# Keys with tokens on partitions: a second read from DRAM in 32-row squares and VectorE's transpose in place of TensorE's

## The chip, the cores and the metric

The kernel runs on one core of a Trainium2 chip. The metric is the device time of one execution in microseconds; lower is better.

## The reference

A layer norm feeds two branches whose outputs are added to the input: a gated delta-rule attention and a small mixture of experts. The change lies in the attention. Cut to what matters:

```python
q = silu(causal_dwconv(x @ Wq));  k = silu(causal_dwconv(x @ Wk)) * DK ** -0.5
v = silu(causal_dwconv(x @ Wv))                        # 16 heads of 128, 2 x 2048 tokens
alpha, beta = sigmoid(x @ Wa + ba), sigmoid(x @ Wb + bb)

def step(S, inps):                                     # one token
    qt, kt, vt, at, bt = inps
    err = einsum('bhvk,bhk->bhv', S, kt) - vt
    S = at[..., None, None] * S - bt[..., None, None] * (err[..., None] * kt[:, :, None, :])
    return S, einsum('bhvk,bhk->bhv', S, qt)

o = layernorm(o) * ln_w + ln_b
o = (o * sigmoid(x @ Wg)) @ Wo
out = x + o + experts(xn)                              # xn: x after the layer norm
```

All arrays are float32.

## The kernel before

The recurrence over tokens is done in chunks of 128 tokens (`C`). A unit `u` is one batch and one pair of heads (`HG` = 2), 16 units in all. A block `n` is 512 tokens of a unit, and has four chunks `c` = 0 to 3. One chunk of one unit is called a step here; there are 16 x 16 = 256 of them. Each has three parts: `before(n, c)` prepares a chunk, `after(n, c)` carries the state `S` across it in the next step, and `output(n, c)` normalises the result one step later still.

Projection and convolution give keys, queries and values with channels on partitions and tokens along the free dimension. `kt` is the key tile of a block, 128 channels x 2 heads x 512 tokens. It was computed well ahead by `key_item`, stored to DRAM in `k_d`, and is read back by `loads`. Most products take it in that layout. The state update is the exception: `after` at L707 needs `kg`, keys with tokens on partitions, scaled for each token by `gd1`. So `before` transposes keys and values for both heads on TensorE with an identity (L640 for keys, L641 for values) into one PSUM bank `pkv`; ScalarE copies the bank to SBUF as `kv` (L649); GpSimd multiplies the key half by `gd1` into `kg` (L655). The value half goes into `r` on VectorE (L691).

Around these lines `before` also builds the inverse of a triangular matrix, in stages that alternate between TensorE (L620, L636, L658, L667) and the other engines. L629 and L631 are VectorE's copies out of the first two PSUM banks, the second with a mask (`pT`). L645 is a transpose on VectorE of a 128 x 32 tile, done in squares of 32 x 32; L646 and L652 place its results.

In `after`, L687 multiplies keys by the state, L691 gives `r`, L698 applies the inverse `inv`, L702 copies the result to `w`, L707 and L714 give the new state, and L721 and L724 write the chunk's output into PSUM. That last pool, `ps_o`, has one bank. In `output`, L748 reads the bank on VectorE, with `rs` that GpSimd computed at L735; only then can the next step's L721 write it.

The steps are interleaved by hand. In `recurrence` a sequence of `step(...)` calls advances the three parts and, between them, two items (`A`, `B`) of the projections of the next block by the plan `PLAN`: q0 and the keys of a later unit at c = 0, q1 and v0 at c = 1, g0 and keys at c = 2, v1 and g1 at c = 3. The items' matmuls are at L155, their convolution sums are three instructions each on VectorE (L141), and `qg` is made on GpSimd (L388) from `gin`, which is loaded into a single buffer (L380). `inv` steps of `inverses` run on GpSimd (L264, L267) out of `Y`, loaded at L255; `ex` steps advance the experts, in the first call of `recurrence` alone. The call is made under a manual schedule:

```python
with tc.manual_schedule(engines={E.PE, E.DVE, E.Activation, E.Pool}):
```

Those four engines run in the written order. DMAs are issued by SyncE (SP) and are placed by the framework's scheduler; each waits for the release of what it overwrites, and on one of eight completion semaphores used in turn. `load_ops` issues 22 small loads for each block (L332, L342, L346), `before` two loads into `inv` (L614), which has four buffers.

`recurrence` is called twice, once for each batch. Between the calls the output projection of the first batch runs by itself; that of the second is interleaved.

Of the kernel before, what the change touches and what calls it, by code (L numbers as in the profile page):

```python
# [7 lines left out]
F32 = mybir.dt.float32  # L8
# [3 lines left out]
ALU = mybir.AluOpType  # L12
# [3 lines left out]
P = 128  # L16
NB, T, HID = 2, 2048, 512
H, D, KS = 16, 128, 4
C = 128
# [5 lines left out]
HG = 2  # L25
NP = H // HG
NHC = HG * NC
Q = 32
NQ = C // Q
# [14 lines left out]
def block_kernel(ctx, tc, x, wq, wk, wv, wg, wo, wa, wb, ba, bb, par, consts,  # L44
                 topk_idx, topk_w, ew0, ew1, ew2, ewd0, ewd1, out):
    nc = tc.nc
# [13 lines left out]
    ident = unit[:, 1:DW]  # L60
# [22 lines left out]
    for i in range(1, NQ, 2):  # L83
# [5 lines left out]
    gd1 = [cp.tile([P, NC, H], F32, tag=f"gd1{b}", name=f"gd1{b}") for b in range(NB)]  # L89
# [25 lines left out]
    k_d = [[dp.tile([HG, P, BLK], F32, name=f"k_d{u}_{k}") for k in range(NBK)]  # L115
           for u in range(NB * NP)]
# [191 lines left out]
    def loads(n):  # L308
# [11 lines left out]
        qg = bp.tile([P, HG, BLK], F32, tag="qg", name="qg")  # L320
        have[n] = (decs, kt, qt, qg, [None] * HG, [])

    def load_ops(n):

        u, blk = blocks[n]
        op = ops[n % 2]
        for h in range(HG):
            hc = slice(h * NC + blk * CB, h * NC + (blk + 1) * CB)
            cc = slice(blk * CB, (blk + 1) * CB)

            def put(k, row, a, q=Q):
                nc.sync.dma_start(out=op[k][row:row + q, :, row:row + q], in_=a)  # L332

            def block(form, g):
                return X_d[u][form, h, g, cc, :].rearrange("c (i j) -> i c j", j=Q)

            for pr in range(2):

                lo, hi, row = 2 * pr, 2 * pr + 1, 64 * h + Q * (1 - pr)
                put("a32", row, aT_d[u][lo * Q:hi * Q, hc, hi * Q:(hi + 1) * Q])  # L340
                put("ihi", row, block(1, hi))
                nc.sync.dma_start(out=op["ilo"][row:row + Q], in_=block(0, lo))  # L342
            for g in range(2):
                row = 64 * h + Q * g
                col = Q * (2 - g)
                nc.sync.dma_start(out=op["top"][row:row + Q, :, col:col + Q], in_=block(0, g))  # L346
                put("bot", 64 * h + Q * g, block(1, 2 + g))
            put("a64", 64 * h, aT_d[u][0:64, hc, 64:C], 64)
# [226 lines left out]
    def bcast(a, n):  # L575
        return bass.AP(a.tensor, a.offset, [*a.ap, (0, n)])

    def v3(t):
        return t.rearrange("p (h j) -> p h j", h=HG)
# [6 lines left out]
    HW = HG * D  # L586
# [16 lines left out]
    def before(n, c):  # L603

        u, blk = blocks[n]
        b = u // NP
        hs = slice((u % NP) * HG, (u % NP) * HG + HG)
        decs, kt, qt, _, vs, _ = have[n]
        op = ops[n % 2]
        ci, cs = blk * CB + c, slice(c * C, (c + 1) * C)  # L610

        inv = invs[(n * CB + c) % len(invs)]
        for g in range(2):
            nc.sync.dma_start(  # L614
                out=inv[g * Q:(g + 1) * Q, :, g * Q:(g + 1) * Q],
                in_=X_d[u][1, :, g, ci, :].rearrange("h (j i) -> j h i", i=Q))


        px = bank(ps_l, "l")
        nc.tensor.matmul(px[:, 0:Q], lhsT=op["a32"][:, c, :], rhs=op["ilo"][:, c, :],  # L620
                         start=True, stop=True)

        pk = bank(ps_l, "l")
        for h in range(HG):
            nc.tensor.matmul(pk[:, h * C:(h + 1) * C], lhsT=kt[:, h, cs], rhs=qt[:, h, cs],  # L625
                             start=True, stop=True)
        yield
        xs = k2.tile([P, Q], F32, tag="xs", name="xs")
        nc.vector.tensor_copy(xs, px[:, 0:Q])  # L629
        pT = k2.tile([P, HG, C], F32, tag="pT", name="pT", bufs=3)  # L630
        nc.vector.scalar_tensor_tensor(  # L631
            pT, v3(pk[:, 0:HW]), D ** -0.5, decs[:, :, c, 1:], ALU.mult, ALU.mult)
        yield

        pz = bank(ps_l, "l")
        nc.tensor.matmul(pz[:, 0:Q], lhsT=op["ihi"][:, c, :], rhs=xs, start=True, stop=True)  # L636

        pkv = bank(ps_l, "l")
        for h in range(HG):
            nc.tensor.transpose(pkv[:, h * D:(h + 1) * D], kt[:, h, cs], ident)  # L640
            nc.tensor.transpose(pkv[:, HW + h * D:HW + (h + 1) * D], vs[h][:, cs], ident)  # L641
        yield
        top, bot = op["top"][:, c, :], op["bot"][:, c, :]
        iT = k2.tile([P, Q], F32, tag="iT", name="iT")
        nc.vector.transpose(iT, pz[:, 0:Q])  # L645
        nc.vector.scalar_tensor_tensor(  # L646
            top[:, 0:Q], pz[:, 0:Q], second[:, 0:1], top[:, 2 * Q:], ALU.mult, ALU.add)
        kv = k2.tile([P, 2, HG, D], F32, tag="kv", name="kv")
        nc.scalar.copy(kv.rearrange("p s h j -> p (s h j)"), pkv)  # L649
        for h in range(HG):  # L650
            r = 64 * h
            nc.scalar.copy(bot[r:r + Q, r + Q:r + 2 * Q], iT[r:r + Q])  # L652
            nc.gpsimd.tensor_copy(inv[0:Q, h, Q:2 * Q], iT[r + Q:r + 2 * Q])  # L653
        kg = k2.tile([P, HG, D], F32, tag="kg", name="kg", bufs=3)
        nc.gpsimd.tensor_tensor(kg, kv[:, 0], bcast(gd1[b][:, ci, hs], D), ALU.mult)  # L655
        yield
        px = bank(ps_l, "l")
        nc.tensor.matmul(px[:, 0:C], lhsT=op["a64"][:, c, :], rhs=wide(top[:, 0:64]), start=True, stop=True)  # L658
        yield
        xs = k2.tile([P, C], F32, tag="xs2", name="xs2")  # L660
        nc.vector.tensor_copy(xs, px[:, 0:C])
        for h in range(HG):
            r = slice(64 * h, 64 * h + 64)
            nc.scalar.copy(inv[64:C, h, 64:C], bot[r, r])
        yield
        pz = bank(ps_l, "l")
        nc.tensor.matmul(pz[:, 0:C], lhsT=xs, rhs=bot, start=True, stop=True)  # L667
        yield
        nc.scalar.copy(inv[0:64, :, 64:C], v3(pz[0:64, 0:C]))
        found[n, c] = (pT, kv, kg, inv)  # L670

    def after(n, c):

# [1 line left out]
        b = u // NP  # L675
        h0 = (u % NP) * HG
        _, kt, _, qg, _, _ = have[n]
        pT, kv, kg, inv = found.pop((n, c))
        ci, cs = blk * CB + c, slice(c * C, (c + 1) * C)
        S = state.get(u)  # L680

        if S is None:
            r = kv[:, 1]
        else:
            pq = bank(ps_c, "c")
            for h in range(HG):
                nc.tensor.matmul(pq[:, h * D:(h + 1) * D], lhsT=kt[:, h, cs], rhs=S[:, h, :],  # L687
                                 start=True, stop=True)
            r = k2.tile([P, HG, D], F32, tag="r", name="r")
            for h in range(HG):  # L690
                nc.vector.scalar_tensor_tensor(  # L691
                    r[:, h, :], pq[:, h * D:(h + 1) * D], gd0[b][:, ci, h0 + h:h0 + h + 1],
                    kv[:, 1, h, :], ALU.mult, ALU.add)
        yield
        yield
        pw = bank(ps_c, "c")
# [66 lines left out]
    def recurrence(b, first):  # L763
# [9 lines left out]
        def step(g):  # L773
            next(g, None)

        inv = last = hold = none
        mine = {}
        with tc.manual_schedule(engines={E.PE, E.DVE, E.Activation, E.Pool}):
            for m, at in enumerate([*steps, None, None]):
                z = after(*steps[m - 1]) if 0 < m <= len(steps) else none  # L780
# [2 lines left out]
                if at:  # L783
                    n, c = at
                    u, blk = blocks[n]
                    ci = blk * CB + c
                    if c == 0:
                        if n + 1 < n0 + NP * NBK:
                            loads(n + 1)
                            load_ops(n + 1)  # L790
                        if blk == 0:
                            for _ in inv:
                                pass
                            inv = inverses(u + 1) if u + 1 < NB * NP else none
                            step(inv)
                    a = before(n, c)
                    for i, (what, h) in enumerate(PLAN[c]):
                        if what == "k":
                            if u + 2 < NB * NP:
                                key = (u + 2, blk, h)  # L800
                                pair[i] = key_item(*key, get_xT if (u + 2) // NP == b else ahead)
                        elif n + 1 < n0 + NP * NBK:
                            pair[i] = item(n + 1, what, h)
                    if u == NB * NP - 1:

                        if ci == 1:
                            wos = load_wo(b)
                        if ci >= 4:
                            if c == 0:
                                slots.append(big())  # L810
                            for _ in last:
                                pass
                            last = out_chunk(b, ci - 4, wos, slots[ci % len(slots)])
                            step(last)
# [311 lines left out]
```

## Time and profile before

| | |
|---|---|
| Time, median of 3 runs (lowest to highest) | 3907.49 us (3904.68 to 3910.80) |
| Profiled execution: its own time, its span | 3906.37 us, 3904.3 us |
| Granted TensorE clock, mean | 0.98 |
| L640, TensorE, 128x128 | 512 of 288 ns mean |
| L641, TensorE, 128x128 | 512 of 272 ns mean |
| L649, ScalarE copy, 128x512 | 256 of 585 ns mean |
| L655, GpSimd multiply, 128x256 | 256 of 616 ns mean |
| L645, VectorE transpose, 128x32 | 256 of 211 ns mean |
| DMAs issued by SyncE | 3390 |

The span runs from the first instruction to the last. [...]

### The profile page before, as it was taken

What the parts mean: (1) busy time and instruction counts of PE and PEld (TensorE: products, weight loads), DVE (VectorE), ACT (ScalarE), POOL (GpSimd) and SP (SyncE); (2) the same over time, 40 slices, a digit from 0 to 9 for tenths busy, and PEclk for the clock granted to TensorE, in tenths of its full rate; (3) what the DMA queues carried; (4) which work ended last, traced back from release to release, by engine and by line L of the source; (5) the groups of instructions that cost most, each with busy time, mean ns of one, the idle gap of its engine ahead of it and who ended that gap; (6) DMA issues with size and microseconds to landing.
All of it is one profiled execution on the core that took longest, in us unless ns stands there. A gap on an engine that the chain in (4) does not pass through costs nothing.

```text
span 3904.3 us, 59006 instructions
## 1 busy us (share of the span) xinstructions
PE 3770.2 (97%) x18046; PEld 2461.4 (63%) x18046; DVE 2343.6 (60%) x6132; ACT 1701.5 (44%) x4027; POOL 1682.4 (43%) x3046
## 2 busy tenths in 40 slices
PE   7769999999999999999999999999999999998899
PEld 6437767677677766666654466666666666664454
DVE  5536656666666667777750177777777777763231
ACT  3424444444444445555520055555555555542110
POOL 1236546465564636363630053636363545541010
PEclk7789999999999999999999999999999999999999
DMA  4634665655666553545573435353435444342322
GB/s 133 209 98 143 185 169 154 195 158 175 168 176 172 159 178 107 143 132 169 147 240 117 120 103 137 107 139 109 132 111 139 119 127 126 103 111 72 100 75 89
DMA packets 579705, 541.36 MB, mean 139 GB/s; under 512 B 354688, under 2 KB 421760, under 8 KB 574272
## 3 DMA queue, kind: packets, MB, share of 16 engines
q1 hardware_dynamic: 557280, 456.18, 40.6%
q0 software_dynamic: 22112, 81.41, 7.1%
q8 instruction: 147, 2.41, 0.3%
q14 instruction: 166, 1.36, 0.1%
HBM read 363.69 MB, written 173.67 MB: 138 GB/s over the span
## 4 chain that ended last, share of the span: by engine, by line
PE 85%; DVE 6%; DMA 4%; issue 2%; POOL 2%; SPq 1%; ACT 1%; POOLq 0%; DVEq 0%; ACTq 0%
PE p L155 39%; PE p L892 11%; PE p L1044 4%; DVE cv L141 3%; PE o L721 3%; PE l L625 3%; PE p L205 3%; PE o L724 3%; PE c L698 3%; PE c L707 3%; PE c L687 2%; PE p L1059 2%; PE l L640 1%; PE l L658 1%; PE l L667 1%
## 5 line engine op out<-in xcount | busy, mean ns | idle before, releaser
L141 DVE SCALAR_TENSOR_TENSOR cv<-raw,prm,cv 128x512 f32<-128x512 f32 x1152 | 909.5, 790 | 106.2 <-ACT cv L136 44.1
L892 PE MATMUL p<-wo,oTf 128*128 128x512 f32 x1024 | 459.7, 604 | 26.3 <-DMA oTf<-oT_d 25.1
L155 PE MATMUL p<-xT,wq 128*128 128x512 f32 x1024 | 484.6, 596 | 0.0
L653 POOL COPY inv<-iT 32x32 f32<-32x32 f32 x512 | 103.1, 201 | 884.4 <-DVE iT L645 685.1
L155 PE MATMUL p<-xT,wg 128*128 128x512 f32 x1024 | 482.0, 594 | 0.0
L155 PE MATMUL p<-xT,wv 128*128 128x512 f32 x1024 | 481.0, 593 | 0.0
L735 POOL TENSOR_TENSOR rs<-rs,mhalf 128x2 f32<-128x2 f32 x256 | 270.2, 1055 | 485.4 <-DVE rs L734 481.1
L132 ACT COPY raw<-p 128x512 f32<-128x512 f32 x384 | 223.4, 582 | 533.2 <-PE p L155 515.0
L155 PE MATMUL p<-xT,wk 128*128 128x512 f32 x896 | 433.5, 610 | 0.0
L702 ACT COPY w<-c 128x256 f32<-128x256 f32 x256 | 95.3, 372 | 635.0 <-PE c L698 635.0
L714 DVE SCALAR_TENSOR_TENSOR S<-S,gtot,c 128x128 f32<-128x128 f32 x480 | 145.2, 344 | 356.6 <-PE c L707 342.5
L892 PEld LDWEIGHTS p<-wo,oTf 128*128 128x128 f32 x1024 | 193.9, 194 | 252.2 <-issue 223.8
L267 POOL TENSOR_TENSOR Y<-Y,t 128x30 f32<-128x30 f32 (+14 forms) x480 | 308.4, 643 | 37.2
L136 ACT ACTIVATE cv<-p,prm 128x512 f32<-128x512 f32 x384 | 300.4, 782 | 1.7
L264 POOL TENSOR_TENSOR t<-Y 128x30 f32<-128x30 f32 (+14 forms) x480 | 286.2, 596 | 8.8 <-DMA Y<-aT_d 2.3
L155 PEld LDWEIGHTS p<-xT,wq 128*128 128x128 f32 x1024 | 178.0, 192 | 135.8 <-issue 135.8
L155 PEld LDWEIGHTS p<-xT,wg 128*128 128x128 f32 x1024 | 176.8, 191 | 132.3 <-issue 132.1
L155 PEld LDWEIGHTS p<-xT,wv 128*128 128x128 f32 x1024 | 176.3, 191 | 132.0 <-issue 132.0
L691 DVE SCALAR_TENSOR_TENSOR r<-c,gd,kv 128x128 f32<-128x128 f32 x480 | 145.3, 344 | 166.2 <-PE c L687 165.1
L155 PEld LDWEIGHTS p<-xT,wk 128*128 128x128 f32 x896 | 160.6, 198 | 126.3 <-issue 126.3
L388 POOL TENSOR_TENSOR qg<-q,gin 128x512 f32<-128x512 f32 x128 | 194.1, 1516 | 98.6 <-ACT q L386 98.6
L707 PEld LDWEIGHTS c<-w,kg 128*128 128x128 f32 x1024 | 154.1, 191 | 121.4 <-issue 102.1
(172 smaller groups left out, 7145.8 us busy)
## 6 DMA issues: line engine op xcount, KB each, us to landing
row<-a_d SPq DMA_DIRECT2D x128, 258.0 KB
dec_d<-decA SPq DMA_DIRECT2D x128, 258.0 KB
decB<-dec_d SPq DMA_DIRECT2D x64, 516.0 KB
k_d<-kf SPq DMA_DIRECT2D x128, 256.0 KB
k<-k_d SPq DMA_DIRECT2D x64, 512.0 KB
gin<-gin_d SPq DMA_DIRECT2D x128, 256.0 KB
aT_d<-aTf SPq DMA_DIRECT2D x128, 256.0 KB
oT_d<-oT SPq DMA_DIRECT2D x256, 128.0 KB
```

The source lines that it names most:

```text
L132: nc.scalar.copy(raw[:, KS - 1:], ps)
L136: nc.scalar.activation(cv, ps, AF.Identity, bias=cbias(p, h0 + h), scale=tap(p, h0 + h, KS - 1))
L141: nc.vector.scalar_tensor_tensor(cv, raw[:, j:j + BLK], tap(p, h, j), cv, ALU.mult, ALU.add)
L155: nc.tensor.matmul(ps, lhsT=w[:, k, h * D:(h + 1) * D], rhs=xt[k], start=(k == 0), stop=(k == NKT - 1))
L264: nc.gpsimd.tensor_tensor(t, bass.AP(col.tensor, col.offset, [col.ap[0], (Q, j), (0, n)]), bass.AP(row.tensor, row.offset, [row.ap[0], (0, ...
L267: nc.gpsimd.tensor_tensor(Y[:, 0:j, j + 1:], Y[:, 0:j, j + 1:], t, ALU.add)
L388: nc.gpsimd.tensor_tensor(qg[:, h, :], qt[:, h, :], gin, ALU.mult)
L691: nc.vector.scalar_tensor_tensor(r[:, h, :], pq[:, h * D:(h + 1) * D], gd0[b][:, ci, h0 + h:h0 + h + 1], kv[:, 1, h, :], ALU.mult, ALU.add)
L707: nc.tensor.matmul(pss[:, h * D:(h + 1) * D], lhsT=kg[:, h, :], rhs=w[:, h, :], start=True, stop=True)
L735: nc.gpsimd.tensor_tensor(rs, rs, mhalf[:, 0:HG], ALU.pow)
L892: nc.tensor.matmul(py, lhsT=oT[:, h, :], rhs=wos[h], start=(h == 0), stop=(h == H - 1))
L1044: nc.tensor.matmul(ps[:fn, s, :], lhsT=w[f][:, s, k, :], rhs=xt[:, k, :], start=(k == 0), stop=(k == NKT - 1))
```

## The change

Keys with tokens on partitions are no longer made by TensorE. The block's keys in `k_d` are read from DRAM a second time, one chunk at a time, into a tile `kb`. For each group `g` of 32 tokens one DMA brings the four 32-channel pieces of both heads, so that the 32 partitions of the group hold channels within a piece, and the free dimension holds head, piece and token. Each square of 32 x 32 is then where it belongs, but turned; one transpose of VectorE, which turns every square by itself, gives `kg`. GpSimd scales `kg` in place. TensorE transposes values alone, and ScalarE copies half as much.

`squares` issues four DMAs per step, each of 32 KB in rows of 128 bytes. It is called two steps ahead in the written order; `kb` has four buffers. The transpose is written behind `pT`, so that it stands between L631 and the next item's instruction on VectorE. The order of the other engines' instructions is the same but for the edited lines; that of SyncE's changes, since the scheduler places the new loads among the others.

```diff
+    def squares(n, c):
+        u, blk = blocks[n]
+        kbs[n, c] = kb = bp.tile([P, HG, D], F32, tag="kb", name="kb", bufs=4)
+        for g in range(NQ):
+            o = c * C + g * Q
+            nc.sync.dma_start(
+                out=kb[g * Q:(g + 1) * Q].rearrange("r h (i j) -> r (h i) j", j=Q),
+                in_=k_d[u][blk][:, :, o:o + Q].rearrange("h (i r) j -> r (h i) j", r=Q))
+
+    kbs = {}
...
         nc.vector.scalar_tensor_tensor(
             pT, v3(pk[:, 0:HW]), D ** -0.5, decs[:, :, c, 1:], ALU.mult, ALU.mult)
+        kg = k2.tile([P, HG, D], F32, tag="kg", name="kg", bufs=3)
+        nc.vector.transpose(kg.rearrange("p h j -> p (h j)"), kbs.pop((n, c)).rearrange("p h j -> p (h j)"))
         yield
...
         for h in range(HG):
-            nc.tensor.transpose(pkv[:, h * D:(h + 1) * D], kt[:, h, cs], ident)
-            nc.tensor.transpose(pkv[:, HW + h * D:HW + (h + 1) * D], vs[h][:, cs], ident)
+            nc.tensor.transpose(pkv[:, h * D:(h + 1) * D], vs[h][:, cs], ident)
...
-        kv = k2.tile([P, 2, HG, D], F32, tag="kv", name="kv")
-        nc.scalar.copy(kv.rearrange("p s h j -> p (s h j)"), pkv)
+        v = k2.tile([P, HG, D], F32, tag="vT", name="vT")
+        nc.scalar.copy(v, v3(pkv[:, 0:HW]))
...
-        kg = k2.tile([P, HG, D], F32, tag="kg", name="kg", bufs=3)
-        nc.gpsimd.tensor_tensor(kg, kv[:, 0], bcast(gd1[b][:, ci, hs], D), ALU.mult)
+        nc.gpsimd.tensor_tensor(kg, kg, bcast(gd1[b][:, ci, hs], D), ALU.mult)
...
+        squares(*steps[0]), squares(*steps[1])
         with tc.manual_schedule(engines={E.PE, E.DVE, E.Activation, E.Pool}):
...
+                    if m + 2 < len(steps):
+                        squares(*steps[m + 2])
                     a = before(n, c)
```

In `after`, `kv[:, 1]` becomes `v`.

More of the change, by code (lines that the diff above doesn't have):

```diff
@@ L669, in before @@
         nc.scalar.copy(inv[0:64, :, 64:C], v3(pz[0:64, 0:C]))
-        found[n, c] = (pT, kv, kg, inv)
+        found[n, c] = (pT, v, kg, inv)
     def after(n, c):
@@ L677, in after @@
         _, kt, _, qg, _, _ = have[n]
-        pT, kv, kg, inv = found.pop((n, c))
+        pT, v, kg, inv = found.pop((n, c))
         ci, cs = blk * CB + c, slice(c * C, (c + 1) * C)
@@ L682, in after @@
         if S is None:
-            r = kv[:, 1]
+            r = v
         else:
@@ L692, in after @@
                     r[:, h, :], pq[:, h * D:(h + 1) * D], gd0[b][:, ci, h0 + h:h0 + h + 1],
-                    kv[:, 1, h, :], ALU.mult, ALU.add)
+                    v[:, h, :], ALU.mult, ALU.add)
         yield
```

## The prediction

> **What bounds the kernel now.** I read the profile page's busy shares first, then the chain of waits, then the two stretches that hold the change (from about 250 to 2000 us and from 2250 to 3820 us, the two calls of `recurrence`), then one step of it in order of time.
>
> ```profile
> span 3904.3 us, 59006 instructions
> PE 3770.2 (97%) x18046; PEld 2461.4 (63%) x18046; DVE 2343.6 (60%) x6132; ACT 1701.5 (44%) x4027; POOL 1682.4 (43%) x3046
> PE 85%; DVE 6%; DMA 4%; issue 2%; POOL 2%; SPq 1%; ACT 1%; POOLq 0%; DVEq 0%; ACTq 0%
> DMA packets 579705, 541.36 MB, mean 139 GB/s; under 512 B 354688, under 2 KB 421760, under 8 KB 574272
> ```
>
> TensorE is busy and also 85% of the chain that ends last. The stretches show how little it pauses where the edited code runs, at a granted clock of 1.00 and 0.99, and how much room the others have:
>
> ```profile
> core 0: us, PE busy (x) PEld busy (x) DVE busy (x) ACT busy (x) POOL busy (x), PEclk, DMA share, GB/s
> 250.00:2000.00 1750.00, 1730.08 (x9144) 1190.39 (x9143) 1143.68 (x2967) 850.12 (x2045) 916.07 (x1587) 1.00 0.56 161
> 2250.00:3820.00 1570.00, 1532.71 (x7326) 989.50 (x7325) 1016.95 (x2737) 745.32 (x1780) 678.05 (x1300) 0.99 0.40 113
> ```
>
> So a TensorE instruction less is worth its issue spacing, not its duration (starts overlap). The timeline of one step (c = 1) gives the spacing; columns are start, duration, engine, line:
>
> ```profile
> 3088.98 0.31 PE L636 MATMUL l<-xs,ihi 128*128 128x32 f32 x2
> 3089.12 0.30 PE L640 MATMUL l<-unit,k 128*128 128x128 f32 x1
> 3089.26 0.27 PE L641 MATMUL l<-unit,v 128*128 128x128 f32 x1
> 3089.38 0.27 PE L640 MATMUL l<-unit,k 128*128 128x128 f32 x1
> 3089.48 0.27 PE L641 MATMUL l<-unit,v 128*128 128x128 f32 x1
> 3089.59 1.88 PE L155 MATMUL p<-xT,wq 128*128 128x512 f32 x4
> 3091.31 0.61 PE L707 MATMUL c<-w,kg 128*128 128x128 f32 x4
> 3092.23 0.49 PE L721 MATMUL o<-w,pT 128*128 128x128 f32 x2 [0.31 <-DVE o L748]
> ```
>
> The four transposes start at 3089.12, .26, .38, .48, and the next work at .59: 0.47 us together, 0.11 us each after the first. The last row is the only place where TensorE pauses in this step: L721 needs the single output bank that VectorE's L748 empties. What VectorE did before it:
>
> ```profile
> 3088.03 0.41 DVE L631 SCALAR_TENSOR_TENSOR pT<-l,decB 128x256 f32<-128x256 f32 x1
> 3088.74 2.54 DVE L141 SCALAR_TENSOR_TENSOR cv<-raw,prm,cv 128x512 f32<-128x512 f32 x3 [0.30 <-POOL raw L131]
> 3091.20 0.20 DVE L645 STREAM_TRANSPOSE iT<-l 128x32 f32<-128x32 f32 x1
> 3091.33 0.20 DVE L646 SCALAR_TENSOR_TENSOR top<-l,second,top 128x32 f32<-128x32 f32 x1
> 3091.46 0.71 DVE L748 TENSOR_SCALAR o<-o,mv,rs 128x128 f32<-128x128 f32 x2
> ```
>
> The new instruction comes right behind L631, ahead of all of these; there is 0.30 us of idle time to take some of it up.
>
> **The change part by part.**
>
> *Removed from TensorE.* 2 transposes (L640) in each of 256 steps. The pair that stays costs the first's 0.14 and one 0.11, so 0.47 falls to 0.25: 0.222 us x 256 = 56.8 us, all on the path. [...]
>
> *ScalarE.* L649 copies 128x256, not 128x512: by L702 (the same copy out of PSUM, 372 ns) against 585 ns, 0.21 us less per step. ScalarE waits for TensorE anyway; worth 0 on the path, but the copies of L652 behind it come that much sooner. *GpSimd.* L655 keeps its size (616 ns) and now waits for VectorE's earlier write rather than for ScalarE; nothing uses kg before L707 of the next step, some 10 us later. 0.
>
> *Added on VectorE.* One 128x256 f32 transpose SBUF to SBUF per step. No row has that size. From below: it could hide wholly (0), if idle time covers it. Near rows: L711, a 128x256 copy out of PSUM, 425 ns; L631, 421 ns; L645, the 128x32 transpose, 211 ns against 180 ns for the 128x32 copy L629, so a square costs about 31 ns more to fill. I take 0.45 us, of which 0.08 overlaps the next start as in neighbouring rows: 0.37 us of occupancy. From above: eight squares at 211 ns each, one after another, 1.69 us (1.6 of occupancy). [...]
>
> *What that does to L721.* For every step I took from the timeline the idle time between L631 and L748, and the slack between L748's end and L721's start (0.06 us of it is the hand-over). Median slack is 1.44 us at c = 0, 0.25 at c = 1 (a tenth have none), 1.18 at c = 2 and 3; idle time averages 0.24 at c = 1, 0.05 to 0.17 at c = 2 and 3, and all is covered at c = 0. TensorE comes 0.222 earlier, so a step gains max(-0.222, delay of L748 - slack). Summed over the steps: occupancy 0.24 us gives -48.7 us, 0.37 gives -44.1 (of it -13.6, -3.9, -13.0, -13.6 for c = 0 to 3), 0.54 about -37, 0.70 -28.5, 1.0 -1, 1.6 +75. VectorE then waits for TensorE at L714 and L661 in most steps (342.5 and 137.6 us in all), so its delay isn't carried over.
>
> *Added on SyncE.* 4 DMAs per step, 1024 more beside 3390. Mean issue is 0.434 us, so 1.7 us per step of about 12, 445 us in all; its issues now take 1473 us of the span. The other queues keep their order but for the edit; SyncE's changes, the squares standing among the loads, often eight together behind a block's 22 small loads. A square waits only for the transpose four steps earlier, which nothing holds up for long. Laying the changed order over the trace's issue times and releases, half of the DMAs issue no later, nine in ten at most 3.1 us, one in a hundred over 8. Against that stands the time from landing to first use now: squares themselves 4 us at the least (39 in the middle), inv 19 us before L698 at least, k 31, bot, top and a 31. Only two are tight: gin ahead of L388 (one buffer; I get 10 of 128 late, 16 us together) and Y ahead of L264 (10 of 16 late, 25 us together). Both hold GpSimd, behind them the rs of L735 that L748 needs; GpSimd idles 3 us and more per step (885 us ahead of L653). I charge +3 us, bounds 0 and 41.
>
> *DMA load.* A square row is 128 bytes: 256 per DMA, 262144 packets more. The trace's packet records hold as many of that size already, median 13 ns: 262144 x 13 ns / 16 engines = 213 us, 5.5% of the span on top of 0.56 and 0.40. The mean packet of SyncE's queue, 45 ns, would make it 19%. [...] Even so no engine fills up: 0, with what delay there is inside the +3.
>
> Sum: -56.8 + 12.7 (VectorE ahead of L721) + 3 = -41 us. The profiled execution lasted 3906.4 us (3904.3 of span and 2.1 around it), 1.1 below the median 3907.5; 3907.5 - 41 = 3866.
>
> **The rivals.**
> 1. *The transpose hides wholly* (filled into VectorE's waits): -57, about 3851. For it: VectorE is busy 65% here. Against: at c = 1 it has only 0.24 us to spare before L748. Chance 0.12.
> 2. *VectorE's transpose is dear, and L748 holds L721 at c = 1, 2 and 3.* It decides from 1.0 us of occupancy on; at 1.6 it is +75, with the +3 about 3985, slower. For it: no row of this size; where GpSimd runs beside them three L141 take 2.54 us instead of 2.33, so something shared exists. Against: the 128x32 row is only 31 ns above a copy, and the rows that stretch so (L141, L759) read two SBUF tensors, the transpose one. Chance 0.12.
> 3. *SyncE lags, and gin and Y reach TensorE through L735:* -44 + 41 = -3, about 3904, no change. For it: the tight slacks. Against: GpSimd's idle time. Chance 0.12, part of the way in half of it.
> 4. *TensorE doesn't get faster because its spacing isn't what paces it.* Against: loads and matmuls of the neighbours both follow at 0.11 us. Below 0.02, within rival 3.
>
> **How the numbers follow.** Main case 0.64: 3866, by itself 3855 to 3880 (occupancy 0.24 to 0.61, lateness 0 to 10). The range takes in rival 1 and the nearer half of rival 3: 3848 to 3899. About 0.2% (8 us) can be told from no change here. Faster by more than that: 0.64 + 0.12 + half of rival 3, 0.82; same 0.06; slower 0.12.
>
> **What would show it.** Right: TensorE 512 matmuls fewer, v's pair followed by the next work at 0.25 us; the new transpose near 0.45 us; the wait of L721 for L748, 11.6 us now, grown to some 15 to 30 us, nearly all at c = 1; squares never waited for. Wrong: a transpose over 1 us; VectorE waiting for kb; GpSimd waiting for gin or Y by tens of us with L748 waiting for rs; or TensorE idle at L698, L625 or L636.

## The result, and the profile after

| | before | after |
|---|---|---|
| Median of five runs (lowest to highest) | 3907.39 us (3903.92 to 3910.80) | 3888.25 us (3882.59 to 3894.72) |
| Profiled execution: its own time, its span | 3906.37 us, 3904.3 us | 3885.77 us, 3884.0 us |

The ratio after to before is 0.9952, with a 95% interval from 0.9938 to 0.9967: 19 us faster, where 41 were forecast. The direction was right, the size less than half.

Line numbers behind L319 grow by 12 to 15 in the changed kernel. The names used below, before and after: L620 is L632, L625 L637, L636 L650, L641 L654, L645 L658, L655 L667, L698 L710, L707 L719, L721 L733, L735 L747, L748 L760, L380 L392, L388 L400. The new transpose is L646, the loads of squares L329. In the versions with more lines the same instructions lie up to six lines away.

From the page after: the span, the busy shares, the packets, and the chain by engine.

```profile
span 3884.0 us, 59363 instructions
...
PE 3722.7 (96%) x17534; PEld 2410.9 (62%) x17534; DVE 2417.6 (62%) x6388; ACT 1653.4 (43%) x4027; POOL 1674.4 (43%) x3046
...
DMA packets 858241, 575.00 MB, mean 148 GB/s; under 512 B 633217, under 2 KB 700289, under 8 KB 852801
...
PE 81%; DVE 6%; DMA 4%; SPq 1%; issue 1%; POOL 1%; ACT 0%; DVEq 0%; POOLq 0%; ACTq 0%
```

TensorE has 512 matmuls less and is busy 47.5 us less, but the span fell by only 20.3 us: TensorE idles 27 us more. Squares' rows show as packets under 512 B: 633217 now, 354688 before. The two stretches of the prediction, after:

```profile
core 0: us, PE busy (x) PEld busy (x) DVE busy (x) ACT busy (x) POOL busy (x), PEclk, DMA share, GB/s
250.00:2000.00 1750.00, 1717.82 (x8921) 1171.25 (x8920) 1183.38 (x3105) 827.91 (x2046) 913.51 (x1591) 0.99 0.64 172
2250.00:3820.00 1570.00, 1523.13 (x7132) 974.03 (x7131) 1057.87 (x2881) 719.11 (x1779) 675.95 (x1302) 0.99 0.48 124
```

In the first stretch TensorE idled 19.9 us before and 32.2 us now, and the granted clock is 0.99, no longer 1.00. The step that the prediction showed (c = 1), in the timeline after (start, duration, engine, line):

```profile
3071.35 0.41 DVE L643 SCALAR_TENSOR_TENSOR pT<-l,decB 128x256 f32<-128x256 f32 x1
3071.68 0.43 DVE L646 STREAM_TRANSPOSE kg<-kb 128x256 f32<-128x256 f32 x1
...
3072.30 0.31 PE L650 MATMUL l<-xs,ihi 128*128 128x32 f32 x2
...
3072.45 0.42 PE L654 MATMUL l<-unit,v 128*128 128x128 f32 x2
...
3072.70 1.88 PE L155 MATMUL p<-xT,wq 128*128 128x512 f32 x4
...
3074.77 0.71 DVE L760 TENSOR_SCALAR o<-o,mv,rs 128x128 f32<-128x128 f32 x2
...
3075.54 0.49 PE L733 MATMUL o<-w,pT 128*128 128x128 f32 x2 [0.52 <-DVE o L760]
```

The pair of values starts at 3072.45 and the next work at 3072.70: 0.25 us, as forecast, where it was 0.47. The transpose takes 0.43 us right behind `pT`. L760 comes 3.42 us after L643's start, as far as L748 came after L631 before (3.43), so VectorE took the transpose up in its own idle time. L733 could have started 0.22 us earlier and does not: its wait grew from 0.31 to 0.52 us. In this step nothing is won. In the others it is; the table compares the starts of L637 in consecutive steps, one profiled execution against the other (256 steps, c is the chunk within its block):

| | after minus before |
|---|---|
| ordinary step, median, c = 0, 2, 3 | -0.218 us |
| ordinary step, median, c = 1 | -0.09 us |
| up to the first step | +1.5 us |
| steps of the first call of `recurrence` | -14.2 us |
| last step of the first call to first of the second (127 to 128) | +8.6 us |
| steps of the second call | -15.5 us |
| behind the last step | -0.7 us |

The sum is the -20.3 us of the spans. An ordinary step thus wins what the prediction says. But seven step distances grew by more than 0.5 us: number 13 by 3.6, 33 by 1.8, 110 by 1.5, 114 by 2.9, 127 by 8.6, 226 by 3.7 and 238 by 4.8, together 26.9 us. Without them the spans would differ by 47 us, about what the forecast has without its charge for SyncE, 44; they are the missing part. The waits show who was late (engine, line, waited for: us in all, times, longest):

```profile
POOL qg L400 <- DMA gin<-gin_d: 31.6, 11, 5.3
...
PE o L733 <- DVE o L760: 29.8, 32, 2.9
...
DVE xgT L1049 <- DMA y_d<-y: 8.2, 5, 3.0
PEld p L907 <- DMA wo<-in_wo: 8.1, 3, 5.0
...
PE p L907 <- DMA wo<-in_wo: 5.6, 3, 4.2
```

The same groups in the kernel before, with no wait for `gin` at all:

```profile
PE o L721 <- DVE o L748: 11.6, 19, 1.8
...
PEld p L892 <- DMA wo<-in_wo: 2.0, 1, 2.0
...
DVE xgT L1034 <- DMA y_d<-y: 1.3, 2, 1.1
PE p L892 <- DMA wo<-in_wo: 1.2, 1, 1.2
```

None of these is a wait for squares, and the transpose L646 never waited for one: `gin`, `y_d` and `wo` are other transfers on SyncE's queue. Of the late steps, 110, 114, 226 and 238 have a long wait for `gin`, 13 and 33 one for `y_d`, 127 those for `wo`. Step 114 shows the way through. `gin` was issued at 1833.36 us, while its buffer had been free since about 1827.1 (the end of the L400 before). In the 6.2 us between, SyncE issued eleven other transfers, three of them squares, and was issuing for 5.5 us of them. From the timeline:

```profile
1840.21 1.26 POOL L400 TENSOR_TENSOR qg<-q,gin 128x512 f32<-128x512 f32 x1 [4.97 <-DMA gin<-gin_d]
...
1841.42 0.18 POOL L131 COPY raw<-halo 128x3 f32<-128x3 f32 x1
...
1841.64 2.35 DVE L141 SCALAR_TENSOR_TENSOR cv<-raw,prm,cv 128x512 f32<-128x512 f32 x3 [3.51 <-POOL raw L131]
...
1844.17 0.71 DVE L760 TENSOR_SCALAR o<-o,mv,rs 128x128 f32<-128x128 f32 x2
...
1844.93 0.49 PE L733 MATMUL o<-w,pT 128*128 128x128 f32 x2 [2.90 <-DVE o L760]
```

GpSimd stands at L400 for 4.97 us. The next item's tiny halo copy L131 is queued behind it; VectorE's convolution L141 needs that copy; L760 is queued behind L141; TensorE's L733 needs L760. The wait ends as 2.90 us of idle TensorE, and is entered under L760, which is not its cause.

### The profile page after: what moved, and what is told of

Read it like the earlier page. It is cut to its first block, busy times and chain, and to the rows that moved or that the text cites. A ratio compares the mean times of both kernels' runs of the same rounds, so it can differ in the third digit from the quotient of the medians.

```text
span 3884.0 us, 59363 instructions
## 1 busy us (share of the span) xinstructions
PE 3722.7 (96%) x17534; PEld 2410.9 (62%) x17534; DVE 2417.6 (62%) x6388; ACT 1653.4 (43%) x4027; POOL 1674.4 (43%) x3046
## 2 busy tenths in 40 slices
DMA packets 858241, 575.00 MB, mean 148 GB/s; under 512 B 633217, under 2 KB 700289, under 8 KB 852801
## 4 chain that ended last, share of the span: by engine, by line
PE 81%; DVE 6%; DMA 4%; SPq 1%; issue 1%; POOL 1%; ACT 0%; DVEq 0%; POOLq 0%; ACTq 0%
PE p L155 38%; PE p L907 11%; PE p L1059 4%; PE o L733 3%; DVE cv L141 3%; PE l L637 3%; PE p L205 3%; PE o L736 3%; PE c L710 3%; PE c L719 2%; PE c L699 2%; PE p L1074 2%; PE l L670 1%; PE l L654 1%; PE l L679 1%
## 5 line engine op out<-in xcount | busy, mean ns | idle before, releaser
L141 DVE SCALAR_TENSOR_TENSOR cv<-raw,prm,cv 128x512 f32<-128x512 f32 x1152 | 896.5, 778 | 99.1 <-ACT cv L136 45.0
L907 PE MATMUL p<-wo,oTf 128*128 128x512 f32 x1024 | 458.6, 602 | 31.9 <-DMA oTf<-oT_d 26.3
L747 POOL TENSOR_TENSOR rs<-rs,mhalf 128x2 f32<-128x2 f32 x256 | 270.6, 1057 | 452.6 <-DVE rs L746 450.4
L907 PEld LDWEIGHTS p<-wo,oTf 128*128 128x128 f32 x1024 | 193.0, 193 | 257.5 <-issue 221.7
L726 DVE SCALAR_TENSOR_TENSOR S<-S,gtot,c 128x128 f32<-128x128 f32 x480 | 145.0, 343 | 293.1 <-PE c L719 292.9
L264 POOL TENSOR_TENSOR t<-Y 128x30 f32<-128x30 f32 (+14 forms) x480 | 287.1, 598 | 7.9 <-DMA Y<-aT_d 1.6
L703 DVE SCALAR_TENSOR_TENSOR r<-c,gd,vT 128x128 f32<-128x128 f32 x480 | 145.2, 344 | 168.9 <-PE c L699 167.6
L400 POOL TENSOR_TENSOR qg<-q,gin 128x512 f32<-128x512 f32 x128 | 193.2, 1510 | 115.9 <-ACT q L398 82.5
L719 PEld LDWEIGHTS c<-w,kg 128*128 128x128 f32 x1024 | 154.1, 191 | 122.3 <-issue 103.4
```

The costliest lines, as they stand in the source:

```text
L141: nc.vector.scalar_tensor_tensor(cv, raw[:, j:j + BLK], tap(p, h, j), cv, ALU.mult, ALU.add)
L264: nc.gpsimd.tensor_tensor(t, bass.AP(col.tensor, col.offset, [col.ap[0], (Q, j), (0, n)]), bass.AP(row.tensor, row.offset, [row.ap[0], (0, ...
L400: nc.gpsimd.tensor_tensor(qg[:, h, :], qt[:, h, :], gin, ALU.mult)
L703: nc.vector.scalar_tensor_tensor(r[:, h, :], pq[:, h * D:(h + 1) * D], gd0[b][:, ci, h0 + h:h0 + h + 1], v[:, h, :], ALU.mult, ALU.add)
L719: nc.tensor.matmul(pss[:, h * D:(h + 1) * D], lhsT=kg[:, h, :], rhs=w[:, h, :], start=True, stop=True)
L747: nc.gpsimd.tensor_tensor(rs, rs, mhalf[:, 0:HG], ALU.pow)
```

## Theories and experiments

Theory A: TensorE's saving and the transpose are as forecast, and the missing 27 us are SyncE's: 1024 more issues in one in-order queue make other transfers late. B: they are the DMA engines', through 262144 packets of 128 bytes. C: the transpose costs more than its delay of L733. D: the single buffer of `gin` binds anyway, with or without squares. Times are medians of each chip's own runs; the ratio comes from all runs and can differ by up to 0.0007 from the quotient of the two medians beside it. Late steps, sums by c and "between" (the distance of steps 127 and 128 against before) are from one profiled execution of each version.

| version | us | before, same chip | ratio (95%) | between |
|---|---|---|---|---|
| squares loaded once | 3856.40 | 3903.34 | 0.9883 (0.9868 to 0.9898) | +1.2 |
| before, with loads only | 3919.68 | 3903.34 | 1.0049 (1.0036 to 1.0063) | +6.5 |
| before, loads an eighth as large | 3915.59 | 3902.66 | 1.0033 (1.0020 to 1.0045) | +8.3 |
| squares on ScalarE's queue | 3934.22 | 3903.34 | 1.0079 (1.0065 to 1.0092) | 0.0 |
| before, `gin` twice | 3903.84 | 3905.12 | 0.9997 (0.9989 to 1.0006) | -0.7 |
| after, `gin` twice | 3872.98 | 3903.34 | 0.9920 (0.9906 to 0.9933) | +8.4 |
| - and transpose twice | 3885.82 | 3905.12 | 0.9954 (0.9941 to 0.9968) | +8.6 |
| - and transpose one stage later | 3879.22 | 3905.12 | 0.9932 (0.9918 to 0.9945) | +10.3 |
| - and two kinds of transfer on ScalarE's queue | 3884.30 | 3905.12 | 0.9948 (0.9934 to 0.9962) | -1.1 |
| - and two chunks in one load | 3852.61 | 3902.66 | 0.9871 (0.9856 to 0.9886) | +5.0 |
| - the same, first pair of each call singly | 3867.31 | 3903.49 | 0.9906 (0.9890 to 0.9923) | +10.0 |

**The squares loaded once.** Four fixed tiles are loaded for the first four chunks and used for all, so 16 loads remain of 1024; every other instruction stays. The keys of later chunks are left out of the state update.

```diff
-        kbs[n, c] = kb = bp.tile([P, HG, D], F32, tag="kb", name="kb", bufs=4)
+        i = (n * CB + c) % 4
+        if i in fixed:
+            kbs[n, c] = fixed[i]
+            return
+        kbs[n, c] = fixed[i] = kb = bp.tile([P, HG, D], F32, tag=f"kb{i}", name=f"kb{i}", bufs=1)
```

> The changed kernel with only the first four chunks' squares ever loaded (16 DMAs instead of 1024); every later step transposes those again, so its keys are left out from the state update. TensorE, VectorE, ScalarE and GpSimd issue the same instructions as the changed kernel. Theory A (SyncE's one queue issues gin, a y_d store and the wo loads late behind the squares): about 3858, some 49 us below before, that is the 0.218 us of the ordinary steps without the few late ones. Theory B (the squares' packets slow the other transfers): the same, 3858. Theory C (the price is VectorE's transpose ahead of L733, more than the 13 us that I gave it): about 3888, as the changed kernel.

Measured: 3856.4 us, -47 us. By c the steps give -15.0, -6.9, -15.5 and -13.9 us (the prediction's working had -13.6, -3.9, -13.0 and -13.6), and no step within the calls is late. One line of its waits:

```profile
PE o L737 <- DVE o L764: 20.2, 28, 2.2
```

So TensorE's saving and VectorE's transpose are worth together what the prediction's sum without SyncE says, -44, and C falls: the transpose runs here too. Of after's wait at L733, 29.8 us, 20 thus come with the transpose; the other 10 are told of below. What remains, 0.9952 against 0.9883, is 27 us for the loads.

**The loads alone.** The kernel before, with `squares` added; a copy of one column by GpSimd stands for their use.

```diff
+        seen = k2.tile([P, 1], F32, tag="seen", name="seen", bufs=1)
+        nc.gpsimd.tensor_copy(seen, kbs.pop((n, c))[:, 0, 0:1])
```

> The kernel before, with the squares loaded on SyncE beside it; nothing uses them but a copy of one column on GpSimd per step, which releases the buffer (pT and kg have two buffers instead of three to make room). TensorE and VectorE as before. A and B: 20 to 29 us above before, 3927 to 3936. C: within 3 us of before.

Measured: +16 us by the medians, +19 (14 to 25) by the ratio, at or a little under the band's lower end. The late steps are of the same kind (114 by 4.0, 127 by 6.5 us). The loads thus cost time without the rest of the change, but less than beside it: in after TensorE is 0.22 us a step faster and leaves all transfers less time, which we read as the reason but did not try by itself. Theory A is supported, B is not excluded.

**The loads an eighth as large.** The same number of issues; each moves one 32 x 32 square and not eight, 32 packets and not 256.

```diff
-                out=kb[g * Q:(g + 1) * Q].rearrange("r h (i j) -> r (h i) j", j=Q),
-                in_=k_d[u][blk][:, :, o:o + Q].rearrange("h (i r) j -> r (h i) j", r=Q))
+                out=kb[g * Q:(g + 1) * Q, 0, 0:Q],
+                in_=k_d[u][blk][0, 0:Q, o:o + Q])
```

> The kernel before with the 1024 loads of the squares added and not used, as in the run before with loads only, but each of these loads moves one square of 32x32 (32 packets of 128 bytes) in place of eight (256 packets). The number of issues on SyncE's queue is the same, the added packets are an eighth. Theory A (what the reload costs is SyncE's time to issue, which makes other transfers late): about what the loads of all squares cost, +13 to +17 us over before (ratio 1.0033 to 1.0044), with the step between the two recurrences 5 to 8 us longer and the wo loads waited for. Theory B (what it costs is the 128-byte packets on the DMA engines): an eighth of it, 0 to +3 us (ratio 1.000 to 1.0008).

Measured: +13 us, interval 8 to 18. With an eighth of the bytes most of the cost is left. B falls, but for the few us that the two intervals allow. The traces agree: from issue to landing (the last count on the transfer's completion semaphore before its next use) `gin` takes 3.74 us in the median before and 4.20 after, `y_d` 3.99 in both, `wo` 4.96 and 5.07. The transfers are little slower; they start later.

What costs is thus what 1024 more transfers bring to one in-order queue. That is three things, which no run takes apart: the time to issue them; waits, since a square whose buffer isn't free holds up all behind it (SyncE waited for L646 52 times in after, 51.5 us in all, and about 65 us for GpSimd's copy in each of the two versions with loads only); and the other order in which the scheduler places the loads. In step 114 hardly any wait is among it: SyncE was issuing for 5.5 of the 6.2 us.

**The squares on ScalarE's queue.** The same packets, issued by another engine.

```diff
-            nc.sync.dma_start(
+            nc.scalar.dma_start(
                 out=kb[g * Q:(g + 1) * Q]
```

> The changed kernel with the squares issued from ScalarE's queue; as many DMAs and packets. A: SyncE's issues stand as before, so gin, y_d and wo come as before: about 3858 plus what four issues per step cost ScalarE (0 to 10 us). B: as the changed kernel, 3888, since the packets are the same. C: 3888.

Measured: +31 us over before. Both halves of the answer are in it. `gin`, `wo` and `y_d` came in time again (no wait for `gin`, nothing lost between the calls), with all packets in place: that is against B and for A. But each issue takes ScalarE about half a microsecond out of its own stream (four in 1.97 us at 1006.32), 439 us in all, and between the issues ScalarE waits: 164 us in the 221 groups of four that have no other work of ScalarE in between, since each issue waits for the transfer ahead of it on its completion semaphore to land. (In the trace of after, SyncE's 4414 transfers are counted on eight such semaphores, 551 or 552 on each, and none is issued before that landing.) All this stands ahead of copies that TensorE needs:

```profile
ACT raw L132 <- DMA kb<-k_d: 149.9, 83, 5.0
ACT g L386 <- DMA kb<-k_d: 147.4, 28, 9.3
...
PE c L719 <- ACT w L714: 29.8, 24, 7.7
```

The columns are as in the waits above. The steps at c = 1 lose 49 us in sum, more than all that was won. Here the place in the queue was the cost, and moving the issues put it nearer to TensorE: 1.0079 of before, where it was 0.9952 from SyncE's queue.

**A second buffer for `gin`**, in the kernel after and, as the control, in the kernel before. To make room `pT` and `kg` go from three buffers to two.

```diff
-            gin = bp.tile([P, BLK], F32, tag="gin", name="gin", bufs=1)
+            gin = bp.tile([P, BLK], F32, tag="gin", name="gin", bufs=2)
```

> The changed kernel with two buffers for gin (two instead of three for pT and kg). A: the wait of L400 for gin, 31.6 us, falls under 5, and the four steps in which L733 idled 1.5 to 2.9 us become ordinary: 12 to 15 us less than the changed kernel, about 3875; the late wo loads and the y_d store stay. B: the same if only gin is late; C: no change, 3888.

> The kernel before with two buffers for gin (two instead of three for pT and kg), no squares. A (gin is late only because the squares stand ahead of it): within 3 us of before, since L388 never waits for gin there. Rival D (a second gin buffer is worth the same without squares, so gin2's gain says nothing on them): 10 to 15 us below before.

Measured: 0.9920 after, 0.9997 before. A second buffer is worth 0.32% or some 12 us where the squares are loaded and nothing where they are not; D falls. All waits for `gin` are gone, and L733's wait for L760 is 20.2 us as with the squares loaded once: the 10 us above that were `gin`'s. The steps left late are 13 by 6.0, 125 by 1.7, 127 by 8.4 and 244 by 1.6. Step 13 shows the second victim, in SyncE's queue (SPq), on VectorE and on TensorE:

```profile
462.57 3.17 SPq L329 DMA_DIRECT2D kb<-k_d  x6
...
466.52 4.04 SPq L626 DMA_DIRECT2D inv<-X_d  x4
...
470.66 0.37 SPq L1079 DMA_DIRECT2D y_d<-y  x1
...
476.05 0.69 DVE L1049 COPY xgT<-p 128x512 f32<-128x512 f32 x1 [4.13 <-DMA y_d<-y]
...
477.10 1.19 PE L710 MATMUL c<-r,inv 128*128 128x128 f32 x4 [3.10 <-issue]
```

The store of the experts' `y` comes behind six squares and the `inv` loads that wait among them. VectorE's copy L1049 needs the buffer that this store frees, r (L703) is queued behind L1049, and TensorE waits for r. The page puts the last row down to "issue"; the cause is three engines back.

**The transpose twice**, beside the second `gin`, to measure VectorE's price by itself.

```diff
-        nc.vector.transpose(kg.rearrange("p h j -> p (h j)"), kbs.pop((n, c)).rearrange("p h j -> p (h j)"))
+        for _ in range(2):
+            nc.vector.transpose(kg.rearrange("p h j -> p (h j)"), kbs[n, c].rearrange("p h j -> p (h j)"))
```

> The changed kernel with two gin buffers and the transpose done twice in a row. By the prediction's table of occupancy (0.35 to 0.70 us) 16 us more than with two gin buffers alone, about 0.996 of before, two thirds of it at c = 1. If VectorE's room hides it: no change from 0.9920. If every step pays it in full: 256 x 0.35 = 90 us more.

Measured: 0.0034 above the version with one, 13 us; the steps at c = 1 went from +0.9 to +14.1 us in sum, the others together from -40.6 to -39.4. The expectation, from the prediction's table of slack, was 16 us, two thirds of it at c = 1. The size holds; the place does not, since it all lies at c = 1.

**The transpose one stage later**, behind L726 and L760 on VectorE, so that L733 wouldn't wait for it.

```diff
-        kg = k2.tile([P, HG, D], F32, tag="kg", name="kg", bufs=2)
-        nc.vector.transpose(kg.rearrange("p h j -> p (h j)"), kbs.pop((n, c)).rearrange("p h j -> p (h j)"))
...
+        yield
+        kg = k2.tile([P, HG, D], F32, tag="kg", name="kg", bufs=2)
+        nc.vector.transpose(kg.rearrange("p h j -> p (h j)"), kbs.pop((n, c)).rearrange("p h j -> p (h j)"))
         nc.gpsimd.tensor_tensor(kg, kg, bcast(gd1[b][:, ci, hs], D), ALU.mult)
-        yield
```

> The changed kernel with two gin buffers, and the transpose and GpSimd's multiply moved one stage on: on VectorE behind L760 and L726, where it waits for TensorE anyway, instead of behind pT. If the price of the transpose is paid at L733, in the c = 1 steps: 8 to 11 us less than with two gin buffers alone (0.9920 of before), about 0.9895 to 0.99 of before, and L733's wait back to about 12 us. If VectorE's work has no part in it: no change from 0.9920.

Measured: 0.9932, against 0.9920 with the transpose where it was: no gain, and a loss that isn't clear of the scatter. The multiply L668 now makes GpSimd wait in another place:

```profile
POOL kg L668 <- PE l L670: 339.8, 130, 6.2
```

The steps at c = 1 lost 5.5 us in sum against before (0.9 where the transpose stands early), and L733's wait is 25.1 us, not 12. The expectation missed. We read it as VectorE relieved at the price of GpSimd's order, which was not tested by itself.

**Stores of `y_d` and loads of `wo` on ScalarE's queue**, beside the second `gin`.

```diff
-            nc.sync.dma_start(out=t, in_=wo[o:o + n * D, :].rearrange("(h p) o -> p h o", p=P))
+            nc.scalar.dma_start(out=t, in_=wo[o:o + n * D, :].rearrange("(h p) o -> p h o", p=P))
...
-        nc.sync.dma_start(out=y_d[i * P:(i + 1) * P, :], in_=y)
+        nc.scalar.dma_start(out=y_d[i * P:(i + 1) * P, :], in_=y)
```

> The changed kernel with two gin buffers, and the y_d stores (31) and wo loads (16) issued from ScalarE's queue instead of SyncE's; the squares stay on SyncE. A: the late y_d store and the late wo loads, 6.0 and 8.4 us of the profile with two gin buffers, come in time: 10 to 14 us less, about 0.9885 of before. Against it: ScalarE waits in its own order for what those DMAs overwrite, as it did with the squares; then nothing is gained, 0.992 or more.

Measured: 0.9948, 11 us worse than without. Between the calls the loss is gone (-1.1 us instead of +8.4), so `wo` was late for SyncE's sake alone. But steps elsewhere grew, 241 by 9.2 us, 12 by 3.0, 32 by 2.6. In step 241 ScalarE issues eight `wo` loads in a row, which take 9.02 us: each of the last four waits until one of the first four has landed, whose completion semaphore it uses again. In step 12 the store of `y_d` is issued 6.3 us after its `y` was ready, when a load of squares that SyncE had issued on the same semaphore has landed. So what stops ScalarE there is not a buffer, as the expectation has it, but a semaphore that other transfers hold. Two of its waits:

```profile
PE l L637 <- ACT inv L681: 8.9, 6, 3.0
...
ACT w L714 <- DMA wo<-in_wo: 8.4, 1, 8.4
```

**Two chunks in one load**, beside the second `gin`: the keys lie chunk by chunk in `k_d`, and one load brings a group's squares of two chunks, 512 loads of 512 packets.

```diff
+        if c % 2:
+            return
+        kb = bp.tile([P, 2, HG, D], F32, tag="kb", name="kb", bufs=2)
+        kbs[n, c], kbs[n, c + 1] = kb[:, 0], kb[:, 1]
...
+                out=kb[g * Q:(g + 1) * Q].rearrange("r x h (i j) -> r (x h i) j", j=Q),
+                in_=k_d[u][blk][c:c + 2, :, :, g * Q:(g + 1) * Q].rearrange("x h (i r) j -> r (x h i) j", r=Q))
```

> The changed kernel with a second buffer of gin, and with the squares of two chunks in one load (the keys lie chunk by chunk in DRAM; 512 loads of squares of 512 packets in place of 1024 of 256; the load of a block's keys takes two issues of 512-byte rows in place of one of 2048). Packets of the squares are as many, SyncE issues about 450 transfers fewer. Theory A (SyncE's issues make y_d's stores and the wo loads late): the step between the recurrences gives back about half of its 8.4 us, step 13 of its 6, in all 3864 to 3869 us on a chip where the version with the second gin buffer takes 3873 (ratio to before 0.9895 to 0.9910). Theory B (packets): no gain, 3872 to 3876 (ratio 0.9915 to 0.993), since the keys' rows are shorter packets besides.

Measured: 3852.6 us, -50 us, the fastest of all versions and 11 us below the band. Part of that is not A's. Its first step begins 17.8 us earlier than in before: the framework's scheduler found another order for TensorE's work ahead of the first recurrence. The rest, -35.6 us, stands against -32.1 with the second `gin` alone: a gain of some 3 us for half the issues, all of it between the calls, which is within the scatter of single executions. To tell the two apart, the same with the first pair of each call loaded singly, which brings the old order back:

```diff
+        k = 1 if (n, c) in steps0 else 2
+        for x in range(0, 2, k):
...
+                    out=kb[g * Q:(g + 1) * Q, x:x + k].rearrange("r x h (i j) -> r (x h i) j", j=Q),
```

> The version with a second buffer of gin and the squares of two chunks in one load, but the very first pair of chunks is loaded by eight single loads. With that the planner orders TensorE's work ahead of the first recurrence as in the kernel before, the changed kernel and the version with the second gin buffer; in the version with all pairs it found another order, and there the first step began 17.8 us earlier than before. Theory O (those 17.8 us belong to the order of the work ahead of the recurrence, and have nothing to do with the keys): the first step begins within 2 us of before, the steps behind it as in the version with all pairs (-35.6 us against before in all), time about 3867 us (3864 to 3870) where before takes 3903, ratio 0.991. Theory P (the single-issue pairs or the keys' chunk by chunk layout bring the start forward): start -15 us or more, time 3852, ratio 0.987.

Measured: 3867.3 us; the first step begins 2.9 us earlier than before (2 were allowed), the rest is -35.8 us, the same sum in other parts: step 13 came in time there (the first call gives -23.0 us, not -17.8), and the time between the calls grew by 10.0. Its ratio, 0.9906, is not clear of the 0.9920 with the second `gin` alone, so what fewer, larger loads are worth stays open. Neither pairs nor layout bring the start forward. That the order does is the one difference left, but the order was not changed by itself.

These versions also show how the time between the calls depends on SyncE's queue. At step 127 loads for the first two or three steps of the second call are placed ahead of the first of the five `wo` loads still to come (three are issued earlier in every version). Its place is read from SyncE's timeline, counted from the start of the step's L637 (in before L625), and set against the distance of steps 127 and 128:

| version | loads of squares ahead of `wo` | `wo` issued at | 127 to 128, against before |
|---|---|---|---|
| before | 0 | 0.9 us | 0 |
| squares loaded once | 0 | 0.8 us | +1.2 us |
| two chunks in one load | 4 | 2.4 us | +5.0 us |
| first pair singly | 8 | 6.9 us | +10.0 us |
| after, `gin` twice | 12 | 7.9 us | +8.4 us |
| after | 12 | 8.6 us | +8.6 us |

In the timeline of after, SyncE's rows:

```profile
1976.67 4.36 SPq L329 DMA_DIRECT2D kb<-k_d  x8
...
1985.01 1.92 SPq L329 DMA_DIRECT2D kb<-k_d  x4
...
1987.98 0.47 SPq L889 DMA_DIRECT2D wo<-in_wo  x1
...
1990.12 1.05 SPq L889 DMA_DIRECT2D wo<-in_wo  x2
```

L907's wait for `wo`, up to 4.2 us in the waits above, follows. The order in the table is rough: with the first pair singly `wo` is issued earlier than in after, but the step distance grew more.

## Why the prediction was right and wrong

- *TensorE's 56.8 us:* right. 0.25 us to the next work, -0.218 us in the median ordinary step.
- *0.11 us apiece:* the timeline's spacing was the right choice against the duration. By an estimate from L640's 288 ns the 512 transposes would have been worth 147 us; the squares loaded once give -47.
- *The transpose at 0.45 us, occupancy 0.37:* right; 425 to 439 ns. *The 12.7 us ahead of L721:* right within a few us, by the squares loaded once (-47 against -44.1) and by the doubling (13 against 16). Its sign that nearly all of L721's wait lies at c = 1 held with the squares loaded once (18.1 of 20.2 us); in after it is 18.2 of 29.8, since late `gin` loads put 9.5 at c = 2.
- *ScalarE and GpSimd at 0:* nothing in the runs speaks against it. L662 takes 372 ns, as the near row said.
- *DMA load at 0:* right. The 128-byte packets took 13.3 ns in the mean, 13.2 before; loads with an eighth of the packets cost 13 us where all cost 16, and `gin`'s landing took 0.46 us longer in the median.
- *The step that failed: "I charge +3 us, bounds 0 and 41".* Measured 27 us (after against squares loaded once), 16 to 19 for the loads alone. The bound held, the value was taken from the wrong end of it. The count of late `gin` loads was good (10 forecast, 11 seen), their length was not (16 us forecast, 31.6 seen). The cover named, GpSimd's idle time, held for seven of the eleven, waits of up to 2.2 us that made no step late by more than 0.5 us. It did not hold for the four of 3.5 to 5.3 us, which cost steps of 1.5 to 4.8 us, 12.9 in all. The 885 us were a sum over all steps, while what counts is the room behind one late `gin`. And in step 114 the way to TensorE was shorter than thought: not through the rs of L735, but through a halo copy of 0.18 us queued behind L388, and VectorE's order. Nor is it so that nothing holds a square up for long: SyncE waited up to 6.5 us for the transpose that frees its buffer.
- *"Only two are tight: gin and Y":* wrong. L264's wait for `Y` did not grow (2.3 us before, 1.6 after). `y_d`'s stores and `wo` were not on the list, which names only loads within a step, and both are rare: a store that frees a buffer, and a load between the two calls. Together they cost no less than `gin`: 14.0 us of after's late steps (13, 33 and 127), and 17.7 us of late steps are left with the second buffer of `gin`.
- *Rival 3* was thus half true, and deserved far more than 0.12. *Rivals 1, 2 and 4* fall: the transpose neither hides wholly nor is dear, and TensorE's spacing is what paces it.
- *The signs named:* L721's wait of 15 to 30 us came out at 29.8 and looked like a hit, but a third of it was `gin`'s. Without the "wrong" sign (GpSimd waiting for `gin` by tens of us) it would have been misread.

## What to carry to other kernels

A transfer that nothing waits for can still cost time, 27 us here: count its issues in the one in-order queue, and list whatever shares that queue, rare stores and loads at phase borders too, with the slack of the tightest one instead of the mean idle time of the engine that will wait. When an engine's order is written by hand, a wait passes to everything queued behind it (in step 114, 4.97 us of GpSimd at L400 to 2.90 us of TensorE at L733), so follow each late transfer through the queues down to TensorE before charging it as covered. A second buffer for the single-buffered victim gave 12 us here. Another engine's queue cost more than it gave (+31 us over before with the squares on ScalarE's), because its issues and their waits stand in that engine's own work. What larger and fewer transfers give was too little to tell from the scatter (0.9906 of before against 0.9920).

## What the runs showed of the hardware

Four of the late steps also had a lower clock. Between about 282 and 3552 us of the execution before, the records show no granted clock below 1.00. After, there are stretches at 0.50 in steps 13, 127, 226 and 238, each 3.4 or 6.8 us long, 23.9 us in all, and all in steps that are late. Within them, consecutive matmuls of 128x128 of one line start 0.21 us apart in the median, at 1.00 in the same part of the trace 0.11 us. All changes of the granted clock in this trace lie whole multiples of 3.41 us apart. Rows of the windows after, 3.41 or 6.82 us long, cut at such changes or whole multiples of 3.41 us from them:

```profile
core 0: us, PE busy (x) PEld busy (x) DVE busy (x) ACT busy (x) POOL busy (x), PEclk, DMA share, GB/s
474.65:478.06 3.41, 1.46 (x5) 0.42 (x4) 1.21 (x4) 0.00 (x0) 0.42 (x2) 1.00 0.83 292
478.06:481.47 3.41, 3.41 (x18) 3.41 (x19) 3.34 (x10) 0.98 (x4) 0.17 (x1) 0.50 0.64 170
1839.98:1843.39 3.41, 2.06 (x8) 0.98 (x6) 1.68 (x3) 0.30 (x1) 3.04 (x5) 1.00 0.69 241
1843.39:1846.81 3.42, 1.88 (x14) 1.64 (x15) 2.46 (x9) 2.27 (x7) 1.86 (x6) 1.00 0.39 74
1846.81:1850.22 3.41, 3.41 (x12) 1.74 (x11) 2.33 (x7) 1.75 (x6) 2.39 (x3) 1.00 0.20 61
1979.92:1983.34 3.42, 2.01 (x14) 1.46 (x12) 3.35 (x9) 1.16 (x3) 1.16 (x1) 1.00 0.50 123
1983.34:1990.16 6.82, 5.17 (x22) 4.80 (x23) 3.61 (x14) 2.37 (x7) 2.16 (x6) 0.50 0.85 182
```

Behind the row with 1.46 us of busy TensorE (step 13) and the one with 2.01 us (step 127) the clock stood at 0.50; behind 2.06 and 1.88 us, in step 114, it stayed at 1.00. Busy time alone does not tell the two apart: 2.01 us came ahead of 0.50 in one place and 1.88 ahead of 1.00 in another, and no run shows what does. Of step 13's 3.6 us, 1.9 are waiting; the other 1.7 are, by an estimate, half of the 3.41 us at 0.50, since matmuls started about twice as far apart there. By the same estimate at most half of 23.9 us, 12 of the 27, can be the clock's; the rest is the waiting itself. The version with squares loaded once has one such stretch too, 6.8 us in step 127.
